# Issuing the first units of a layer stack beside the last pairs of the stage before it, with memory pools split by lifetime and weight loads moved to another queue

## The chip, the cores and the metric

The kernel runs on one core of a Trainium2 chip. The time is device time in microseconds (us). The core has five engines, each with its own in-order queue of instructions: TensorE (PE, matrix products; its weight loads are listed apart as PEld), VectorE (DVE), ScalarE (ACT), GpSimd (POOL) and SyncE (SP), which issues DMAs. ACT can issue DMAs too. All order between engines comes from semaphores: an instruction at the head of a queue waits, and everything behind it on that engine waits as well.

## What is computed

The input x is 16 sequences of 256 tokens by 128 features, in float32. Four residual blocks follow, cut here to what matters:

```python
x = x + attention(layernorm(x))        # 16 heads of 8, causal softmax
x = x + mixture(layernorm(x))          # per sequence: 2 of 8 rank-64 experts
x = x + retention(layernorm(x))        # 4 heads, decay matrix, rms norm, silu gate
x = x + stack(layernorm(x))            # 6 layers
# stack, per layer:
#   x = local_attention(shift(x)) + x  # 16 heads of 64, window 32, q and k normalised and rotated
#   x = feed_forward(shift(x)) + x     # layer norm, gelu gate
```

## The kernel before

**First stage.** The first three blocks work on pairs of sequences, 8 pairs (class First, g = 0 to 7). Each method is one step of a pair: `st`, `rs`, `z`, `tr`, `zt` (L184 to L227) are the layer norm and the transposition, with a letter for the block (a, m, r, and s for the stack's input); `pr`, `na`, `dq` (L234 to L248) project q and k and bring them into head order by way of DRAM; `sc` to `ov` (L266 to L387) are the attention; `oat` to `ax` (L389 to L404) its output projection and the addition to `xn`; `mxz` to `am` (L408 to L512) the mixture; `rpq` to `ar` (L516 to L678) the retention. `st` with letter s also saves xn to DRAM (`kept`, L186), and `zt` with letter s writes the pair into `xs` (L227), which the stack works on.

**Stack.** 6 layers by 16 sequences make 96 units (class Unit). A unit's steps are `pqk`, `sq`, `t2`, `rot`, `add` (L899 to L927: q and k of head group G, their squares, the rotation), `nr`, `rnA` to `rnC`, `bcD`, `norm` (L931 to L974: norms of q and k, broadcast through DRAM), `pv`, `vc`, `vs` (values), `s`, `sm`, `mx`, `sub`, `exp`, `su`, `rec`, `nm` (scores and softmax), `pt`, `pTc`, `o`, `oTc`, `y`, `xsu` (output). Class Forward does the feed-forward of a pair.

**Order.** Both stages run in an order that is written out by hand: the lists FIRST (L785) and ORDER (L1252). A word such as `oat:-1` is a step and an offset: in round j it is done for pair j - 1 (in ORDER, for unit 2j - 1). All steps are issued in this order, each to its engine's queue, so the list fixes every queue. FIRST is run for j = -8 to 15, and only then ORDER for j from -3, so the first stage's last rounds hold only steps of pairs 6 and 7, and the stack's first rounds only steps of units 0 to 3.

**Memory.** All first-stage tiles live in four pools (`xp`, `ew`, `wk`, and PSUM pools), opened together in one block (L727) and closed together after FIRST. The stack's pools `lw`, `kc`, `s2` (L818 to L820) take the same memory afterwards: `lw` holds weights of q and k, values' weights and rotation tables, `kc` the other weights, the ring of q and k tiles and the values, `s2` the working tiles.

**Loads.** SP loads the 8 tiles of x (L732); ACT loads constants and weights of the first stage, 15 DMAs (L126, L749, L753, L709), in program order ahead of ACT's first computation. POOL makes the scaled rotation tables a half at a time during FIRST (`tab`, L720), SP moves them. The stack's weights for layer 0 are issued by SP at L1299 to L1304; those of later layers by `follow` (L1277). Fills of tiles for attention (qT, kT, vals, less) stand at L758 to L775.

Of the kernel before, what the change touches and what calls it, by code (L numbers as in the profile page):

```python
# [105 lines left out]
_EARLY = ["mask0", "rcos", "rsin", "decay", "expand", "before"]  # L106
_LATE = ["ident", "band", "gather"]
# [3 lines left out]
def kernel(ctx: ExitStack, tc: tile.TileContext, a: dict, widths: dict, out: bass.AP):  # L111
# [12 lines left out]
    def load_consts(pool, names, array):  # L124
        whole = pool.tile([P, sum(widths[n] for n in names)], F32, name=f"c_{names[0]}")
        nc.scalar.dma_start(out=whole, in_=array)  # L126
        got, at = {}, 0
        for n in names:
            got[n] = whole[:, at : at + widths[n]]
            at += widths[n]  # L130
        return got

    c = load_consts(const, _LATE, a["late"])
    ident = c["ident"]
# [3 lines left out]
    def transposed(z, name):  # L138

        ps = bank(ps_tr, f"tr_{name}")  # L140
        for k in range(4):
            nc.tensor.transpose(ps[:, k * P : (k + 1) * P], z[:, k, :], ident)
        return ps
# [16 lines left out]
    class First:  # L160
# [9 lines left out]

        def bank(self, what, *n):
            return self.tile(ps_tr, [P, 512], what, *n, tag=ps_tr.name)
# [8 lines left out]
        def t_z(self, K):  # L181
            return self.wk([P, 4, D], "z", K, tag="ln_za" if K == "a" else "ln_z", bufs=1 if K == "a" else 2)

        def st(self, K):  # L184
            if K == "s":
                nc.sync.dma_start(out=kept[self.g], in_=xn[self.g])  # L186
            st, mv = self.wk([P, 4, 6], "ln_st", K, bufs=4), self.mv(K)
            for k in range(4):
                nc.vector.bn_stats(st[:, k, :], xn[self.g][:, k, :])
                nc.vector.bn_aggr(mv[:, k, :], st[:, k, :])  # L190

# [25 lines left out]
        def zT(self, K):  # L217
            return self.wk([P, 512], "zT", K, tag=f"zT_{K}", bufs=1)
# [18 lines left out]
        def nat(self, x):  # L237
            return self.wk([P, 512], "nat", x, tag=f"nat_{x}", bufs=1)
# [11 lines left out]
        def pav(self):  # L250
            zT = self.zT("a")
            for k in range(4):
# [26 lines left out]
        def mx(self, s, ch, r):  # L279
            for tt in range(2):  # L280
                cols = slice(P, 3 * P) if tt else slice(0, P)
                junk = self.wk([P, 2 * P], "a_junk", s, ch, r, tt, bufs=1)
# [19 lines left out]
        def qS(self, s, ch):  # L302
            return self.wk([P, T], "a_qS", s, ch)
# [23 lines left out]
        def e(self, s, ch, half):  # L327
            return self.wk([P, 3, 2, P], "a_pe", s, ch, half, bufs=4)
# [33 lines left out]
        def oT(self, s):  # L362
            return self.wk([P, 4, T], "a_oT", s)
# [14 lines left out]
        def ov(self, s, tt):  # L378
            p3 = self.bank("ta", s, tt).rearrange("t (h d) -> t h d", d=32)
            rec = self.wk([P, H0, 1], "a_rec", s, tt)  # L380
# [135 lines left out]
        def rpq(self, s):  # L516
            for tt in range(2):
# [188 lines left out]
    def scale_tables(pool):  # L706

        qks = pool.tile([P, DEPTH, 2, 2], F32, tag="qks", bufs=1, name="qks")
        nc.scalar.dma_start(out=qks, in_=a["qks"].rearrange("p (l k h) -> p l k h", l=DEPTH, k=2))  # L709
# [16 lines left out]
    xn = []  # L726
    with ExitStack() as early:  # L727
        xp = early.enter_context(tc.tile_pool(name="xp", bufs=1))
        ew = early.enter_context(tc.tile_pool(name="ew", bufs=1))
        for g in range(NPAIR):  # L730
            xt = xp.tile([P, 4, D], F32, name=f"xn{g}")
            nc.sync.dma_start(out=xt, in_=x_tok[g])  # L732
            xn.append(xt)
        w = load_consts(ew, _EARLY, a["early"])
        for name, shape, src in (
            ("wq", [P, P], a["wq0"]),
            ("wk", [P, P], a["wk0"]),
            ("wv", [P, P], a["wv0"]),
            ("wo", [P, P], a["wo0"]),
            ("wr", [P, NE], a["wr"]),  # L740
            ("wa", [P, 4, D], a["wa"].rearrange("(c p) h -> p c h", p=P)),
            ("wb", [P, 4, D], a["wb"].rearrange("(c p) h -> p c h", p=P)),
            ("wqk", [P, 2 * P], a["wqk1"]),
            ("wvg", [P, 4 * P], a["wvg1"]),
            ("wo1", [P, 2, D], a["wo1"].rearrange("(c p) n -> p c n", p=P)),
            ("gn", [P, 1], a["gn"]),
        ):
            w[name] = ew.tile(shape, F32, name=f"w_{name}")
            nc.scalar.dma_start(out=w[name], in_=src)  # L749


        w["ninth"] = ew.tile([P, 1], F32, name="ninth")
        nc.scalar.dma_start(out=w["ninth"], in_=a["ninth"])  # L753
        headed = {}
        for name in ("wq", "wk"):
            headed[name] = [dram.tile([P, 512], F32, name=f"heads_{name}{n}") for n in range(2)]
        w["qT"], w["kT"] = [], []
        for n in range(2):  # L758
            for kind in ("qT", "kT"):
                t = ew.tile([P, 4, 512], F32, name=f"a_{kind}{n}")  # L760
                if kind == "qT":
                    nc.vector.memset(t, 0.0)
                else:
                    nc.vector.tensor_copy(
                        t.rearrange("p c n -> p (c n)"), w["ninth"].to_broadcast([P, 4 * 512])
                    )
                w[kind].append(t)
        w["vals"] = ew.tile([P, 4, H0, 32], F32, name="vals")
        nc.gpsimd.memset(w["vals"][:, :, :, D0:], 0.0)
        nc.gpsimd.memset(w["vals"][:, :, :, D0 : D0 + 1], 1.0)  # L770
        w["less"] = []
        for n in range(2):
            t = ew.tile([P, 2, 4, 4, 32], F32, name=f"less{n}")
            nc.gpsimd.memset(t, 0.0)
            w["less"].append(t)  # L775

        nc.scalar.mul(w["gn"], w["gn"], 0.5)
        ps_s = early.enter_context(tc.tile_pool(name="ps_sa", bufs=1, **psum))
        ps_p = early.enter_context(tc.tile_pool(name="ps_pa", bufs=1, **psum))
        ps_tr = early.enter_context(tc.tile_pool(name="ps_ma", bufs=2, **psum))  # L780
        wk = early.enter_context(tc.tile_pool(name="wk", bufs=2))
# [3 lines left out]
        FIRST = """  # L785
        dc.1.1:-2 ex.1.3.0:-1 rs.a:2 sp.1.3.1:-1 wt.1.0:-2 af.1.2.1:-1 wt.1.1:-2 mx.0.2.1:0 ex.1.3.1:-1 os.1.0:-2
        oa.1.2:-1 os.1.1:-2 af.1.3.1:-1 af.1.3.0:-1 mx.0.2.0:0 sp.0.0.1:0 oa.1.3:-1 nd.1:-2 oc.1.2:-1 npw.0:-2 pav:0
        oc.1.3:-1 dv.1.0:-1 vlc:0 mx.0.2.2:0 tr.a:1 mx.0.2.3:0 ov.1.0:-1 ex.0.0.1:0 gm.0.0:-2 dv.1.1:-1 sc.0.3:0
        sp.0.0.0:0 ov.1.1:-1 mx.0.3.1:0 nmu.0:-2 zt.a:1 mx.0.3.2:0 tab.0:0 ex.0.0.0:0 gm.1.0:-2 mt.0.2:0 oat:-1
        sh.0.2:0 mx.0.3.3:0 mt.0.1:0 sh.0.1:0 onc:-1 ya:-1 mx.0.3.0:0 sp.0.1.0:0 ex.0.1.0:0 af.0.0.1:0 gm.1.1:-2  # L790
        npw.1:-2 ax:-1 sc.1.0:0 nmu.1:-2 st.m:-1 af.0.0.0:0 ont.0:-2 ont.1:-2 mx.1.0.1:0 af.0.1.0:0 onm.0:-2 rs.m:-1
        onm.1:-2 sp.0.2.1:0 yr:-2 ex.0.2.1:0 z.m:-1 tr.m:-1 sp.0.1.1:0 zt.m:-1 mx.1.0.0:0 mx.1.0.2:0 ar:-2 pl:-1 lg:-1
        oa.0.0:0 pr.q:1 mx.1.0.3:0 sc.1.1:0 af.0.2.1:0 ex.0.1.1:0 oc.0.0:0 mxz:-1 sp.0.2.0:0 ch1:-1 exq:-1 ch2:-1
        mx.1.1.0:0 st.s:-2 pg:-1 na.q:1 mx.1.1.3:0 gt:-1 dq.q:1 pe:-1 gc:-1 wg:-1 pr.k:1 na.k:1 mt.0.3:0 pm:-1
        ex.0.2.0:0 z.a:2 sh.0.3:0 mx.1.1.1:0 rs.s:-2 mt.1.0:0 sh.1.0:0 af.0.1.1:0 mx.1.1.2:0 mix:-1 tab.1:0 ym:-1
        z.s:-2 oa.0.1:0 sp.0.3.1:0 ex.0.3.1:0 af.0.2.0:0 am:-1 oa.0.2:0 st.r:-1 sp.0.3.0:0 sc.1.2:0 rs.r:-1 oc.0.1:0
        mx.1.2.0:0 oc.0.2:0 ex.0.3.0:0 z.r:-1 mt.1.1:0 sp.1.0.0:0 tr.r:-1 sh.1.1:0 dq.k:1 tr.s:-2 mx.1.2.2:0 zt.r:-1
        af.0.3.0:0 mx.1.2.3:0 af.0.3.1:0 mx.1.2.1:0 pvg.0:-1 zt.s:-2 rpq.0:-1 tv.0:-1 gg.0:-1 rt.0:-1 sc.1.3:0
        pvg.1:-1 mx.1.3.3:0 mx.1.3.1:0 pvg.2:-1 ex.1.0.0:0 tv.1:-1 gg.1:-1 ra.0:-1 tv.2:-1 sp.1.0.1:0 oa.0.3:0
        ex.1.0.1:0 oc.0.3:0 gg.2:-1 rpq.1:-1 rqt.0:-1 rqc.0:-1 sp.1.1.0:0 af.1.0.1:0 mx.1.3.0:0 mx.1.3.2:0 af.1.0.0:0  # L800
        rt.1:-1 raw.0.0:-1 sc.0.0:1 ex.1.1.0:0 sp.1.1.1:0 ex.1.1.1:0 dc.0.0:-1 raw.0.1:-1 dc.0.1:-1 wt.0.1:-1
        mx.0.0.2:1 os.0.1:-1 oa.1.0:0 mt.1.2:0 oc.1.0:0 af.1.1.0:0 mx.0.0.1:1 mx.0.0.3:1 tab.2:0 mx.0.0.0:1 ra.1:-1
        sh.1.2:0 rqt.1:-1 gm.0.1:-1 pvg.3:-1 rqc.1:-1 mt.1.3:0 st.a:3 sp.1.2.0:0 sh.1.3:0 tv.3:-1 ex.1.2.0:0
        af.1.2.0:0 af.1.1.1:0 sc.0.1:1 gg.3:-1 wt.0.0:-1 sp.1.2.1:0 mt.0.0:1 os.0.0:-1 mx.0.1.0:1 mx.0.1.1:1 dv.0.1:0
        sh.0.0:1 ex.1.2.1:0 ov.0.1:0 dv.0.0:0 ov.0.0:0 mx.0.1.2:1 oa.1.1:0 sp.1.3.0:0 oc.1.1:0 mx.0.1.3:1 raw.1.0:-1
        sc.0.2:1 dc.1.0:-1 nd.0:-1 raw.1.1:-1
        """.split()
        pairs = [First(g) for g in range(NPAIR)]
        tables = scale_tables(wk)
        with tc.manual_schedule():  # L810
            next(tables)
            for j in range(-8, NPAIR + 8):
# [565 lines left out]
```

## Time and profile before

| what | value |
|---|---|
| median of 3 timed runs | 4303.77 us (4298.45 to 4316.04) |
| profiled execution, its own time | 4305.45 us |
| its span, first to last instruction | 4303.7 us |
| TensorE busy, whole span | 4048.4 us (94%), 100320 matmuls |
| VectorE busy | 2947.2 us (68%) |
| ScalarE busy | 2077.9 us (48%) |
| GpSimd busy | 2525.9 us (59%) |
| mean granted TensorE clock | 0.964 |
| chain that ended last, by engine | PE 74%, DVE 6%, DMA 6%, POOL 4%, ACT 3%, issue 3%, SPq 3% |
| DMA read from HBM, written | 140.98 MB, 17.83 MB |

How to read it: the profile covers one execution. A row of a timeline or group gives the start, the duration, the engine, the source line, the operation and the tiles (output <- input); in brackets stands how long the engine had been idle and what released it. ACTq and SPq are DMA issues on ACT's and SP's queues. PEclk is the share of full speed that TensorE's clock was granted. A wait for several semaphores is put down to the one that came last by the profile. Matmul ends are modelled, so a busy PE is not a PE at its peak.

### The profile page before, as it was taken

Reading aid. Unit: us, or ns where it says so; the run is one execution under the profiler, and the core shown is the slowest. Engines: PE = TensorE matmul, PEld = TensorE weight load, DVE = VectorE, ACT = ScalarE, POOL = GpSimd, SP = SyncE. Lnnn points to the kernel's source line nnn. Section 1 sums busy time; section 2 is a strip of 40 time slices with the busy share of each in tenths; the row PEclk is TensorE's granted clock in tenths of the full one; section 3 lists DMA queues with packets and bytes.
Section 4 is the critical chain, followed back from the end, with each engine's and each line's share of the span. In section 5 each row is a group of like instructions: output and inputs, shape, how many; then the busy total and the mean of one; then the engine's idle time right before and its main releaser. Section 6 shows DMA issues by size and latency. Waiting matters only on the chain.

```text
span 4303.7 us, 216382 instructions
## 1 busy us (share of the span) xinstructions
PE 4048.4 (94%) x100320; PEld 2778.6 (65%) x100320; DVE 2947.2 (68%) x5436; ACT 2077.9 (48%) x3342; POOL 2525.9 (59%) x1419
## 2 busy tenths in 40 slices
PE   5999967999999999999999999999999999999998
PEld 3666654666666666666666666666666666666664
DVE  4677635677777677777777676766767776767764
ACT  2555532445554455544555544544554554445543
POOL 2454536666666666666666666666656666656661
PEclk9999977899999999999999999999999999999999
DMA  3111101222222222222222212222222222222221
GB/s 88 52 36 53 36 34 52 69 59 64 56 73 49 71 59 65 69 64 74 60 65 57 69 48 74 59 64 69 61 49 69 67 57 69 64 64 68 59 63 46
DMA packets 208899, 260.84 MB, mean 61 GB/s; under 512 B 54142, under 2 KB 164604, under 8 KB 207100
## 3 DMA queue, kind: packets, MB, share of 16 engines
q1 hardware_dynamic: 204796, 243.38, 22.1%
q8 instruction: 786, 12.88, 1.3%
q10 hardware_dynamic: 3200, 3.62, 0.3%
q14 instruction: 117, 0.96, 0.1%
HBM read 140.98 MB, written 17.83 MB: 37 GB/s over the span
## 4 chain that ended last, share of the span: by engine, by line
PE 74%; DVE 6%; DMA 6%; POOL 4%; ACT 3%; issue 3%; SPq 3%; ACTq 0%; POOLq 0%; DVEq 0%
PE pqk L902 14%; PE s L1014 11%; PE o L1092 9%; PE pv L980 8%; PE y L1111 5%; DMA v<-v 5%; PE nr L936 4%; PE pt L1069 3%; PE fy L1220 3%; PE fa L1203 3%; PE fg L1190 3%; POOL qk L974 2%; PE p L319 2%; SPq L967 1%; SPq L996 1%
## 5 line engine op out<-in xcount | busy, mean ns | idle before, releaser
L927 POOL TENSOR_TENSOR qk<-qk,t 128x1024 f32<-128x1024 f32 x384 | 907.3, 2366 | 303.1 <-DVE qk L921 301.9
L974 POOL TENSOR_TENSOR qk<-qk,bc 128x1024 f32<-128x1024 f32 x384 | 947.2, 2484 | 75.4 <-DMA v<-v 63.4
L1045 POOL TENSOR_TENSOR sm<-sm,mx 128x1024 f32<-128x1024 f32 x192 | 367.2, 1912 | 975.4 <-DVE mx L1041 291.8
L902 PE MATMUL pqk<-xs,wqk 128*128 128x256 f32 x3072 | 852.8, 406 | 23.0 <-ACT sq L910 12.3
L1014 PEld LDWEIGHTS s<-qk 32*32 32x32 f32 x49152 | 537.8, 104 | 400.5 <-issue 375.4
L910 ACT ACTIVATE sq<-pqk 128x512 f32<-128x512 f32 x768 | 454.6, 599 | 690.0 <-DVE qk L921 361.9
L916 DVE TENSOR_TENSOR t<-pqk,rot 128x512 f32<-128x512 f32 x768 | 521.9, 686 | 298.7 <-ACT sq L910 146.9
L921 DVE TENSOR_TENSOR qk<-pqk,rot 128x512 f32<-128x512 f32 x768 | 515.4, 682 | 278.0 <-PE pqk L902 222.7
L1014 PE MATMUL s<-qk 32*32 32x64 f32 x49152 | 667.8, 223 | 19.5 <-issue 7.6
L902 PEld LDWEIGHTS pqk<-xs,wqk 128*128 128x128 f32 x3072 | 547.8, 195 | 149.2 <-issue 50.1
L1092 PEld LDWEIGHTS o<-pT,v 64*64 64x64 f32 x24576 | 423.2, 139 | 295.0 <-issue 164.8
L1092 PE MATMUL o<-pT,v 64*64 64x32 f32 x24576 | 474.5, 224 | 78.4 <-DMA v<-v 76.3
L1077 ACT COPY pT<-pt 128x512 f32<-128x512 f32 x384 | 224.8, 586 | 449.1 <-PE pt L1069 238.2
L980 PE MATMUL pv<-wv,xs 128*64 128x512 f32 x1536 | 423.1, 630 | 0.0
L1063 DVE TENSOR_TENSOR sm<-sm,rec 128x1024 f32<-128x1024 f32 x192 | 404.2, 2105 | 0.0
L1111 PE MATMUL y<-oT,wo 128*128 128x256 f32 x1536 | 386.8, 396 | 0.3 <-ACT pT L1077 0.3
L1030 DVE TENSOR_TENSOR sm<-s,c_ident 128x1024 f32<-128x1024 f32 x192 | 234.1, 1219 | 148.7 <-PE s L1014 147.7
L1111 PEld LDWEIGHTS y<-oT,wo 128*128 128x128 f32 x1536 | 282.0, 193 | 43.9 <-ACT f_gl L1196 0.8
L1104 ACT COPY oT<-o 128x512 f32<-128x512 f32 x384 | 216.3, 590 | 164.1 <-PE o L1092 164.1
L989 ACT COPY v<-pv 128x512 f32<-128x512 f32 x384 | 224.7, 585 | 127.6 <-PE pv L980 127.5
L1053 DVE TENSOR_REDUCE su<-sm 128x16 f32<-128x1024 f32 x192 | 232.6, 1211 | 41.2 <-ACT sm L1049 41.2
L1069 PE MATMUL pt<-c_ident,sm 128*128 128x128 f32 x1536 | 249.3, 285 | 1.2 <-DVE f_res L1247 0.8
(187 smaller groups left out, 4983.6 us busy)
## 6 DMA issues: line engine op xcount, KB each, us to landing
bc<-ndr SPq DMA_DIRECT2D x768, 128.0 KB
v<-v SPq DMA_DIRECT2D x576, 128.0 KB
v<-v SPq DMA_DIRECT2D x192, 64.0 KB
rot_l<-in_rot_dram SPq DMA_DIRECT2D x12, 512.0 KB
rot<-rot_l SPq DMA_DIRECT2D x12, 512.0 KB
wqk<-in_wqk_dram SPq DMA_DIRECT2D x24, 256.0 KB
rot<-rot SPq DMA_DIRECT2D x6, 1024.0 KB
wv<-in_wv_dram SPq DMA_DIRECT2D x6, 512.0 KB
```

The costliest lines, as they stand in the source:

```text
L902: nc.tensor.matmul(self.p_qk(G, k)[:, hf, :], lhsT=weights["qk", G, self.l][:, k, hf, :], rhs=xq, start=True, stop=True)
L910: nc.scalar.activation(self.squares(G)[:, k], self.p_qk(G, k), AF.Square)
L916: nc.vector.tensor_tensor(self.t_2(G)[:, k], self.p_qk(G, k)[:, ::-1, :], weights["rot", self.l][:, 1, k], ALU.mult)
L921: nc.vector.tensor_tensor(self.qk_t[G][:, k, :, WIN : WIN + T], self.p_qk(G, k), weights["rot", self.l][:, 0, k], ALU.mult)
L927: nc.gpsimd.tensor_tensor(to, to, self.t_2(G), ALU.add)
L974: nc.gpsimd.tensor_tensor(to, to, self.bcast()[:, G, :, None, :].to_broadcast([P, 2, 2, T]), ALU.mult)
L980: nc.tensor.matmul(self.misc("pv", i)[64 * p : 64 * p + 64, :], lhsT=xs[self.g][:, self.seq, cols], rhs=weights["v", self.l][:, p, :], sta ...
L1014: nc.tensor.matmul(ps[32 * b : 32 * b + 32, r2, tt, G // 2, G % 2, :], lhsT=qk[G][rows, 0, hf, WIN + at : 2 * WIN + at], rhs=keys, start=( ...
L1063: nc.vector.tensor_tensor(s3, s3, self.t_rec(hu)[:, :, None].to_broadcast([P, 16, 2 * WIN]), ALU.mult)
L1069: nc.tensor.transpose(pt[:, j * P : (j + 1) * P], sm[:, j // 2, tt, j % 2].rearrange("n p c -> n (p c)"), ident)
L1092: nc.tensor.matmul(o[64 * e : 64 * e + 64, p, 2 * hu + m, WIN * b : WIN * b + WIN], lhsT=self.v_t[rows, 1 - b % 2, 2 * tt + b // 2, 4 * hu ...
L1111: nc.tensor.matmul(self.misc("y")[:, 0:T], lhsT=weights["o", self.l][:, ch, :], rhs=self.t_oT()[:, ch, :], start=(ch == 0), stop=(ch == 7),)
```

## The change

It does four things.

1. **Pools by lifetime.** What only the first attention uses (the x tiles of pairs 0 to 5, wq, wk, wv, mask0, qT, kT, vals, less, z, zT and nat of letter a, a_junk, a_qS, a_pe, a_oT, a_rec, rot_l) goes into pools `ea` and `aw`, the rest of the first stage stays in `ew` and `wk`. `ea`, `aw` and the attention's two PSUM pools are closed after the last attention step, and the stack's `lw` and `s2` are opened in their place, at the other end of memory. The ring of q and k moves into `lw`; values' weights, odd layers' rotation table, vals, wo, w1, w2 and vecs are in `kc`, a few working tiles in the new `s3`; both open when `ew` and `wk` close. The two-bank PSUM pool `ps_m` is opened at the start and serves both stages.
2. **A bridge.** FIRST runs up to the last attention step (`ov.1.1` of pair 7). The 104 steps left, of pairs 6 and 7, are issued in a new list BRIDGE together with 116 steps of units 0, 1 and 2. `ORDER` then skips what has been issued.
3. **Loads.** ACT issues only ident, ninth and mask0 (and no vecs later); SP issues x of pair 0, wq, wk, wv, x of pairs 1 and 2, then the rotation table. The other tiles of x and all other weights and constants of the first stage are issued by SP when `pav` of pair 0 is issued (`load_rest`).
4. **Fills.** Three of the four fills of qT and kT come after `st.a` of pair 0 (`set_heads`); the halving of gn comes at pair 0's `rpq`.

The core of the diff:

```diff
         def st(self, K):
...
+            if K == "a" and self.g == 0:
+                set_heads()
...
         def pav(self):
             zT = self.zT("a")
+            if self.g == 0:
+                load_rest()
...
         def rpq(self, s):
+            if self.g == 0 and s == 0:
+
+                nc.scalar.mul(w["gn"], w["gn"], 0.5)
...
+    early = ExitStack()
+    attention = ExitStack()
+    ew = early.enter_context(tc.tile_pool(name="ew", bufs=1))
+    wk = early.enter_context(tc.tile_pool(name="wk", bufs=2))
+    ea = attention.enter_context(tc.tile_pool(name="ea", bufs=1))
+    aw = attention.enter_context(tc.tile_pool(name="aw", bufs=2))
+    ps_s = attention.enter_context(tc.tile_pool(name="ps_sa", bufs=1, **psum))
+    ps_p = attention.enter_context(tc.tile_pool(name="ps_pa", bufs=1, **psum))
...
+    xn = [(ea if g < NPAIR - 2 else ew).tile([P, 4, D], F32, name=f"xn{g}") for g in range(NPAIR)]
+    nc.sync.dma_start(out=xn[0], in_=x_tok[0])
+    load(ea, nc.scalar, "ninth", [P, 1], a["ninth"])
+    load(ea, nc.scalar, "mask0", [P, 3 * P], a["mask0"])
+    load(ea, nc.sync, "wq", [P, P], a["wq0"])
+    load(ea, nc.sync, "wk", [P, P], a["wk0"])
+    load(ea, nc.sync, "wv", [P, P], a["wv0"])
+    nc.sync.dma_start(out=xn[1], in_=x_tok[1])
+    nc.sync.dma_start(out=xn[2], in_=x_tok[2])
+
+    def load_rest():
+
+        for g in range(3, NPAIR):
+            nc.sync.dma_start(out=xn[g], in_=x_tok[g])
+        load(ew, nc.sync, "wo", [P, P], a["wo0"])
+        load(ew, nc.sync, "wr", [P, NE], a["wr"])
+        w.update(load_consts(ew, _EARLY, a["early"]))
...
+        c.update(load_consts(const, _LATE, a["late"]))
...
+    nc.vector.memset(w["qT"][0], 0.0)
+
+    def set_heads():
         for n in range(2):
...
+            if n:
+                nc.vector.memset(w["qT"][n], 0.0)
+            nc.vector.tensor_copy(
+                w["kT"][n].rearrange("p c n -> p (c n)"), w["ninth"].to_broadcast([P, 4 * 512])
+            )
...
+    firsts = [
+        (method, args, j + d) for j in range(-8, NPAIR + 8) for method, args, d in parse(FIRST) if 0 <= j + d < NPAIR
+    ]
+    mine = ("sc", "mx", "mt", "sh", "sp", "ex", "af", "oa", "oc", "dv", "ov")
+    split = 1 + max(n for n, (method, _, _) in enumerate(firsts) if method in mine)
+
+    with tc.manual_schedule():
+        next(tables)
+        for method, args, g in firsts[:split]:
+            getattr(pairs[g], method)(*args)
+    del firsts[:split]
+    assert next(tables, None) is None
+    attention.close()
...
+    right = dict(side="right")
+    lw = ctx.enter_context(tc.tile_pool(name="lw", bufs=1, **right))
+    s2 = ctx.enter_context(tc.tile_pool(name="s2", bufs=2, **right))
...
+    BRIDGE = """
+        pqk.1.0:0 first.nmu.0:6 first.oat:7 pqk.1.1:0 t2.1.0:0 first.onc:7 first.gm.1.0:6 first.ya:7 first.gm.1.1:6
+        sq.1.1:0 t2.1.1:0 first.npw.1:6 rot.1.0:0 first.ont.0:6 first.ax:7 first.onm.0:6 rot.1.1:0 sq.1.0:0 pqk.0.1:0
+        pqk.0.0:0 first.st.m:7 first.nmu.1:6 first.ont.1:6 rot.0.1:0 sq.0.1:0 first.rs.m:7 first.onm.1:6 t2.0.1:0
+        first.yr:6 add.1:0 t2.0.0:0 first.z.m:7 pqk.3.1:0 rot.0.0:0 first.ar:6 sq.3.1:0 first.tr.m:7 first.mxz:7
+        sq.0.0:0 rot.3.1:0 pqk.3.0:0 t2.3.1:0 first.zt.m:7 first.pl:7 sq.3.0:0 pqk.2.1:0 add.0:0 t2.3.0:0 first.lg:7
+        first.ch1:7 t2.2.1:0 first.exq:7 rot.3.0:0 first.ch2:7 first.st.s:6 first.pg:7 first.gt:7 first.pe:7
+        first.gc:7 rot.2.1:0 pqk.2.0:0 sq.2.1:0 first.wg:7 sq.2.0:0 t2.2.0:0 rot.2.0:0 nr.0:0 first.rs.s:6 first.pm:7
+        add.3:0 pqk.1.1:1 first.mix:7 first.z.s:6 nr.1:0 rnA:0 pqk.0.0:1 t2.1.1:1 first.ym:7 rnB:0 rnC:0 first.am:7
+        bcD:0 sq.0.0:1 rot.1.1:1 sq.1.1:1 pqk.1.0:1 add.2:0 first.st.r:7 rot.0.0:1 first.rs.r:7 t2.0.0:1 t2.1.0:1
+        rot.1.0:1 pqk.0.1:1 first.z.r:7 add.1:1 sq.1.0:1 pqk.3.1:1 rot.0.1:1 first.tr.r:7 first.tr.s:6 first.zt.r:7
+        first.zt.s:6 first.pvg.0:7 norm.1:0 t2.0.1:1 rot.3.1:1 first.tv.0:7 first.rpq.0:7 sq.0.1:1 first.gg.0:7
+        norm.0:0 pqk.3.0:1 first.rt.0:7 first.pvg.1:7 t2.3.0:1 first.tv.1:7 first.pvg.2:7 t2.3.1:1 first.ra.0:7
+        rot.3.0:1 sq.3.1:1 s.0.0.0:0 first.gg.1:7 first.tv.2:7 add.0:1 first.rpq.1:7 sq.3.0:1 first.gg.2:7 pqk.2.1:1
+        first.rt.1:7 first.rqt.0:7 sq.2.1:1 pqk.2.0:1 norm.3:0 first.rqc.0:7 sq.2.0:1 first.ra.1:7 first.raw.0.0:7
+        first.dc.0.0:7 norm.2:0 s.0.1.0:0 t2.2.1:1 first.raw.0.1:7 rot.2.1:1 pqk.1.0:2 first.dc.0.1:7 first.wt.0.1:7
...
+        rnA:1 rnB:1 rnC:1 pqk.1.1:2 s.0.0.1:0 s.0.1.1:0 first.nmu.1:7 sm.0:0 bcD:1 s.1.0.0:0 add.3:1 first.ont.1:7
+        t2.1.0:2 sq.1.1:2 s.1.1.0:0 first.onm.1:7 t2.1.1:2 first.yr:7 rot.1.0:2 mx.0:0 add.2:1 s.1.0.1:0 rot.1.1:2
+        sq.1.0:2 first.ar:7 s.1.1.1:0 sub.0:0 pqk.0.1:2 first.st.s:7 exp.0:0 first.rs.s:7 norm.0:1 first.z.s:7
...
+    """.split()
...
     with tc.manual_schedule():
         for G in range(4):
             weights["qk", G, 0] = load_qk(0, G)
         weights["rot", 0] = load_rot(0)
+        for word in BRIDGE:
+            ((method, args, u),) = parse([word])
+            if method == "first":
+                getattr(pairs[u], args[0])(*args[1:])
+                firsts.remove((args[0], args[1:], u))
+            else:
+                getattr(units[u], method)(*args)
+                issued.add((u, method, *args))
+        assert not firsts
+    early.close()
+
+    kc = ctx.enter_context(tc.tile_pool(name="kc", bufs=1))
+    s3 = ctx.enter_context(tc.tile_pool(name="s3", bufs=2))
...
+    nc.sync.dma_start(out=vecs, in_=a["vecs"].rearrange("p (l n) -> p l n", l=DEPTH))
...
+    with tc.manual_schedule():
         weights["v", 0] = load_v(0)
...
             for method, args, d in parse(ORDER):
                 u = 2 * j + d
-                if 0 <= u < len(units):
+                if 0 <= u < len(units) and (u, method, *args) not in issued:
```

## The prediction

> All positions are microseconds in the profiled execution of before; that run took 4305.45 (span 4303.7), 1.7 above the median 4303.77 of the three timed runs, so differences carry over to the median unchanged.
>
> **What bounds the kernel now.** First the page's slices, because they show where TensorE is not the bound.
>
> ```profile
> PE   5999967999999999999999999999999999999998
> ...
> PEclk9999977899999999999999999999999999999999
> DMA  3111101222222222222222212222222222222221
> ```
>
> A slice is 107.6. PE is below nine tenths in the first slice, in the sixth and seventh (538 to 753), and at the end; its clock sags at the same places. So I asked for busy times by stage (columns: length, PE, weight loads, DVE, ACT, POOL, then granted clock, DMA share, GB/s).
>
> ```profile
> 0.00:20.00 20.00, 0.00 (x0) 0.00 (x0) 6.64 (x18) 0.00 (x0) 7.61 (x25) 1.00 0.98 293
> ...
> 568.00:640.00 72.00, 43.64 (x264) 31.44 (x263) 21.01 (x68) 21.45 (x54) 25.58 (x41) 0.70 0.05 15
> 640.00:706.50 66.50, 45.11 (x856) 30.90 (x856) 29.95 (x46) 15.85 (x25) 34.28 (x15) 0.76 0.27 82
> 706.50:746.00 39.50, 29.93 (x802) 20.64 (x801) 23.47 (x32) 14.00 (x21) 26.03 (x13) 0.80 0.23 53
> 746.00:800.00 54.00, 51.28 (x1432) 35.70 (x1428) 33.31 (x42) 23.37 (x38) 34.61 (x15) 0.83 0.16 41
> 800.00:4200.00 3400.00, 3310.03 (x90211) 2263.07 (x90208) 2434.74 (x3563) 1702.82 (x2596) 2135.93 (x957) 0.98 0.25 64
> ```
>
> From 800 on PE is busy 97% of the time: the stack is bound by TensorE and the change leaves its work as it is. Two stages are bound by latency. In 568 to 640 only the tail of pairs 6 and 7 runs, one dependent step after another; in 640 to 706.5 only the first units run, again a chain. No engine is busy over 68% in either. The first 20 have no matmul at all while DMA is at 0.98. Third, the timeline of ACT over the start, and of SP and ACT at the seam:
>
> ```profile
> 1.26 0.55 ACTq L126 DMA_DIRECT2D c_mask<-in_early_dram  x1
> ...
> 10.47 0.39 ACTq L749 DMA_DIRECT2D w_wq<-in_wq_dram  x1
> ...
> 20.38 0.44 ACTq L709 DMA_DIRECT2D qks<-in_qks_dram  x1
> 20.86 1.28 ACT L202 ACT_TABLE_LOAD   x1 [20.86 <-DMA w_wqk<-in_wqk_dram]
> 22.15 0.50 ACT L202 ACTIVATE z_a<-xn,ln_nb_a,ln_rs_a 128x128 f32<-128x128 f32 x1
> ...
> 637.47 1.13 ACT L227 COPY xs<-tr_s 64x256 f32<-64x256 f32 x3
> ```
>
> ACT issues loads until 20.8, and pair 0's first normalisation stands behind them in its queue, though its operands (POOL's L197) are ready at 9.25. At the other end, pair 7's last copy to xs ends at 638.6.
>
> ```profile
> 636.62 1.96 SPq L851 DMA_DIRECT2D wqk<-in_wqk_dram  x4
> 638.64 0.41 SPq L857 DMA_DIRECT2D rot<-rot  x1
> ...
> 641.31 3.60 PE L902 MATMUL pqk<-xs,wqk 128*128 128x256 f32 x8 [4.25 <-DMA wqk<-in_wqk_dram]
> ...
> 646.28 1.29 DVE L916 TENSOR_TENSOR t<-pqk,rot 128x512 f32<-128x512 f32 x2 [13.49 <-DMA wv<-in_wv_dram]
> ```
>
> SP issues the stack's weights only at 636.62, when ACT's z_s (ending 636.5), the last reader of xn, is done: the new pool waited for the whole old pool. First matmul 4.7 after the issue, first rotation 9.7 after it.
>
> **The start.** ACT keeps three small loads (ident, ninth, mask0), so its queue is free at about 2.5, and the table load is over by 4. What then holds z_a is x's first tile. It landed at 5.5, beside 1760 KB of constants; alone, by the nearest row (a 256 KB write of nat_q, issue 68.54, next step 70.56) it takes 2 to 3, so 3.8. Statistics 1.7 (5.50 to 7.19), POOL's four small steps 2.0 (7.28 to 9.25): z_a at 7.8, at worst 9.3. Gain 14.3 or 12.9; I take 14. The rest of that chain (22.15 to 38.98, first scores) is unchanged: set_heads puts 2.36 + 1.76 + 2.36 = 6.5 of DVE work behind pair 0's statistics, done at about 12, before the heads' DMA needs kT (now about 17) and pair 1's statistics are used. Attention's tiles only change their pool; buffer counts stay: nothing. The postponed loads (4,320 of the 6,060 KB, 15 at 293 GB/s) go to SP behind pair 0's heads, about 23 to 39; next on SP is pair 1's nat_q at 68.5 - 14 = 54. Cover 15; without it, up to 15 on that one DMA. Scaling gn costs 0.19 on ACT: nothing.
>
> [...] The row says more: between 1.8 and 10.47 ACT issued nothing while the transfers drained, and this blocked compute too. What counts is that two thirds of the bytes, and their waits, no longer stand ahead of z_a. I go by the row: 14.
>
> **The seam.** Attention's last read of its pools is ov.1.1 of pair 7, ending at 568.2. SP has nothing else queued (its last table write is at 544.7), so wqk and rot issue at 568.2 instead of 636.6: first matmul 572.9, first rotation 577.5 (rot now follows wqk directly). POOL's ring memsets, 1.2, wait for the same point. The order is static, so this wait has others behind it: on PE pair 7's oat behind pqk.1.0 (4.7 lost); on DVE pair 7's add to xn (ax) behind two t2 and a rot. ax was at 570.5 and goes to 577.5 + 3 x 0.65 = 579.5: the tail's chain starts 9 late.
>
> From there the chain is as before (570.5 to 638.6, 68), but each step also waits for unit work put ahead of it on its engine. Sums of what the bridge issues, from durations in these stages at full clock: PE 31 for units + 30 for pairs = 62; POOL 35 + 27 = 62 (14 adds and norms at 2.36 are 33); DVE 30 + 22 = 52; ACT 17 + 20 = 37. None is near 90, so the chain stays the limit. Walking it, delay against before grows thus: ax 9; ch1 11 (pqk.3.0 ahead of the router's product, t2 and rot on DVE); mix 12; am 13.5 (pqk.1.1, nr.1, pqk.0.0 ahead of ym, a PSUM bank held for the norms); tr.r 16 (pqk.3.1 waits for sq.1.0, which stands behind z.r); ra.0 16.5 (norm.1 and norm.0 ahead on POOL: they wait for the broadcast, 9 from rnC at 667.9 to norm at 676.9, which is about what the chain takes from am to ra.0, so this costs little); raw.0.1 21 (behind s.0.1.0, which waits for norm.2); ont.1 24 (nr.1, three groups of scores, one of them after sm.0 because its PSUM tile has one buffer, then a Sqrt table load of 1.28); the end 24. So pair 7 ends at 638.6 + 24 = 663.
>
> [...] The rows differ: 0.70 at 61% busy, 0.76 at 68%, but still only 0.83 at 95% busy (746 to 800). At 0.8 PE's 62 are 77; about half of PE's work is on the chain: +8. I take +4, between: 667.
>
> Then the second new wait. vecs and wv go into pools that open only when pair 7's is closed: issued at about 666, landed 4.7 later (the wqk row), so PE holds at pv.0 of unit 0 until 671, with everything behind it on PE. pv.0 and pv.3 take 2, and pqk.3.1 of unit 2 starts at 673. Before, the same instruction came at 706.5, also with these two pv done. Gain 33.5; POOL and DVE, which don't wait for wv, are then a few us further ahead (add.1 of unit 2 at about 668 against 706.7), worth 0 to 4. I take 34. SP issues wo and ff right behind (2.5 of issue, ahead of unit 2's broadcast, which is some 20 later); they land long before use: nothing. Steady state: same instructions, buffers and PSUM banks: nothing.
>
> Sum: -14 - 34 = -48: 4305.45 - 48 = 4257.5 by the profiled run, 4256 by the median.
>
> **Rivals.**
> 1. Loads find free memory before 568 or the clock stays full: the 9 at ax vanish, or the 4. Gain up to 14 + 47 = 61: 4243. For it: the free bytes at the top of memory aren't in the trace. Against: before's wqk waited for a whole pool.
> 2. The bridge's in-order queues cost more than my walk: 45 hops at 0.4 more each, 18. Gain 14 + 16 = 30: 4274.
> 3. The seam gives nothing and only the start remains: 4290. This is so if pair 7 ends at 701 or later.
> 4. Slower: the stack's first values, output weights and feed-forward must wait for pair 7's very end, because their pools lie where its tiles are. If the mixed queues lengthen that chain from 68 to 135 (1.5 more at each of 45 hops, as with a POOL add of 2.36 ahead of two steps in three), it ends at 714 and the start's gain is used up: break-even. At 736 it is slower by 0.5% (21.5, about what a measurement can tell from no change): 4326. Against it: only 14 adds and norms exist, and they total 33.
>
> **How the numbers follow.** My forecast (4256, within 4247 to 4265) 0.5; rival 1 0.17; rival 2 0.2; rival 3 0.08; rival 4 0.05. Faster by over 0.5% is below 4282: 0.87; within 0.5% 0.08; slower 0.05. The range takes in rivals 1 and 2: 4238 to 4278.
>
> **What would show it.** z_a at 8 to 9.5 and first scores near 25; wqk issued within 1 of pair 7's last ov, at about 554 on the new time axis; ax about 9 after where it stood relative to that; pair 7's last copy to xs some 95 to 100 after it; PE waiting about 5 for wv at the first pv; from there on the old timeline, 48 early. I'd be wrong if first-stage time between first scores and ov changed (529 now), if the stretch 800 to 4200 changed, or if the chain grew by a POOL or PSUM wait that I priced at nothing.

## The result, and the profile after

The changed kernel takes 4277.4 us (median of 5 runs, 4273.91 to 4286.27) against 4303.77 (5 runs, 4298.45 to 4317.93): ratio 0.9935, 95% interval 0.991 to 0.9959. The gain is 26 us, 18 to 39 by the interval; 48 was forecast. The profiled execution took 4277.4, its span is 4275.7.

First the slices of the changed kernel's page. TensorE in slice 1 rose from 5 to 6 tenths, in the dip of slices 6 and 7 from 6 and 7 to 7 and 8:

```profile
PE   6999978999999999999999999999999999999998
```

The same columns by stage (length, PE, weight loads, DVE, ACT, POOL, granted clock, DMA share, GB/s) for the start and the mixed tail:

```profile
0.00:20.00 20.00, 5.40 (x8) 1.89 (x8) 8.73 (x20) 5.90 (x12) 11.37 (x25) 1.00 0.34 102
557.70:654.50 96.80, 71.45 (x1112) 55.11 (x1112) 50.50 (x116) 37.83 (x80) 56.30 (x53) 0.84 0.19 51
```

The DMA share at the start fell from 0.98 to 0.34, and GpSimd's busy time rose from 7.61 to 11.37 with the same 25 instructions: that is the first thing not forecast. In the mixed tail TensorE is busy 74% of the time at a granted clock of 0.84; before, the same place had 61% at 0.70.

The timeline of the start in the changed kernel shows where GpSimd's time went:

```profile
5.61 1.20 DVE L792 COPY a_kT<-w_ninth 128x2048 f32<-128x2048 f32 x1
5.78 1.11 POOL L203 TENSOR_SCALAR ln_rs_a<-ln_mv_a 128x4 f32<-128x4 f32 x1 [1.01 <-DVE ln_mv_a L197]
6.97 3.93 POOL L204 TENSOR_TENSOR ln_rs_a<-ln_rs_a,mhalf 128x4 f32<-128x4 f32 x1
7.18 1.76 DVE L791 MEMSET a_qT<- 128x2048 f32 x1 [0.37 <-issue]
8.86 1.17 DVE L792 COPY a_kT<-w_ninth 128x2048 f32<-128x2048 f32 x1
11.55 1.65 ACT L211 ACTIVATE z_a<-xn,ln_nb_a,ln_rs_a 128x128 f32<-128x128 f32 x4 [6.22 <-POOL ln_nb_a L206]
```

Two operations on 128 x 4 elements take 1.11 and 3.93, while DVE runs the three moved fills; before, with no fill beside them, the same two took 0.23 and 1.04:

```profile
7.28 0.23 POOL L194 TENSOR_SCALAR ln_rs_a<-ln_mv_a 128x4 f32<-128x4 f32 x1 [2.51 <-DVE ln_mv_a L190]
7.60 1.04 POOL L195 TENSOR_TENSOR ln_rs_a<-ln_rs_a,mhalf 128x4 f32<-128x4 f32 x1
```

So z_a starts at 11.55 (22.15 before), not at 7.8.

The seam, on the changed kernel's timeline:

```profile
557.92 1.78 SPq L871 DMA_DIRECT2D wqk<-in_wqk_dram  x4
...
567.98 1.29 DVE L935 TENSOR_TENSOR t<-pqk,rot 128x512 f32<-128x512 f32 x2 [10.25 <-PE ont L221]
569.78 0.67 DVE L240 TENSOR_TENSOR xn<-xn,ya 128x512 f32<-128x512 f32 x1
...
653.02 1.50 ACT L236 COPY xs<-tr_s 64x256 f32<-64x256 f32 x4
...
653.47 0.42 SPq L882 DMA_DIRECT2D wv<-in_wv_dram  x1
...
657.58 3.68 PE L999 MATMUL pv<-wv,xs 128*64 128x512 f32 x8 [4.60 <-DMA wv<-in_wv_dram]
```

wqk is issued 0.2 after the last ov ends at 557.73. Pair 7's addition (the xn row) starts 12.0 after that end, and its last copy to xs ends 96.8 after it. TensorE then waits 4.60 for wv. The forecast had 11.3, 98.8 and 5 for these three.

What was not: in the stack TensorE's one large wait grew. The waits of PE between the first pT copy of unit 8 and that of unit 92 (us in total, times, longest), before:

```profile
PE o L1092 <- DMA v<-v: 65.5, 80, 3.5
```

and after:

```profile
PE o L1111 <- DMA v<-v: 82.9, 89, 3.8
```

Both executions, cut at four marks (the end of the last ov, and the first copy to pT of units 0, 8 and 92), with a second trace of each kernel taken later (us):

| stretch | before | after | gain | before again | after again | gain |
|---|---|---|---|---|---|---|
| start to last ov | 568.2 | 557.7 | 10.5 | 570.6 | 556.1 | 14.5 |
| to unit 0 | 147.9 | 109.4 | 38.5 | 150.6 | 109.3 | 41.3 |
| to unit 8 | 303.4 | 299.1 | 4.3 | 294.6 | 300.1 | -5.5 |
| to unit 92 | 3124.6 | 3155.5 | -30.9 | 3117.3 | 3121.1 | -3.8 |
| to the end | 159.6 | 154.0 | 5.6 | 151.5 | 153.9 | -2.4 |
| span | 4303.7 | 4275.7 | 28.0 | 4284.7 | 4240.5 | 44.2 |

Start and seam gave what was promised, and more; 31 of it was lost between units 8 and 92 in the first pair of traces, 4 in the second.

### The profile page after: what moved, and what is told of

Read it like the earlier page. It is cut to its first block, busy times and chain, and to the rows that moved or that the text cites. A ratio compares the mean times of both kernels' runs of the same rounds, so it can differ in the third digit from the quotient of the medians.

```text
span 4275.7 us, 216376 instructions
## 1 busy us (share of the span) xinstructions
PE 4036.9 (94%) x100320; PEld 2776.4 (65%) x100320; DVE 2940.5 (69%) x5436; ACT 2077.0 (49%) x3344; POOL 2527.3 (59%) x1419
## 4 chain that ended last, share of the span: by engine, by line
PE 68%; DMA 9%; DVE 8%; POOL 6%; ACT 4%; issue 3%; SPq 3%; POOLq 0%; ACTq 0%; DVEq 0%
PE pqk L921 13%; PE s L1033 10%; PE o L1111 9%; PE pv L999 7%; DMA v<-v 6%; PE y L1130 5%; PE nr L955 4%; PE fy L1239 3%; PE pt L1088 3%; POOL qk L993 3%; PE fg L1209 2%; PE fa L1222 2%; PE p L330 2%; DVE sm L1082 1%; SPq L986 1%
## 5 line engine op out<-in xcount | busy, mean ns | idle before, releaser
L1111 PE MATMUL o<-pT,v 64*64 64x32 f32 x24576 | 480.0, 225 | 94.8 <-DMA v<-v 91.8
L1049 DVE TENSOR_TENSOR sm<-s,c_band 128x1024 f32<-128x1024 f32 x192 | 233.9, 1218 | 145.2 <-PE s L1033 144.2
L1088 PE MATMUL pt<-ident,sm 128*128 128x128 f32 x1536 | 247.1, 284 | 1.8 <-issue 1.0
```

Of the source, the lines that this page charges most:

```text
L1088: nc.tensor.transpose(pt[:, j * P : (j + 1) * P], sm[:, j // 2, tt, j % 2].rearrange("n p c -> n (p c)"), ident)
L1111: nc.tensor.matmul(o[64 * e : 64 * e + 64, p, 2 * hu + m, WIN * b : WIN * b + WIN], lhsT=vals[self.u % 2][rows, 1 - b % 2, 2 * tt + b // 2 ...
```

## Experiments

The experiments ran in four later comparisons, in which the kernel before took 4275.8 to 4286.1 instead of 4303.77; so ratios, and differences within a comparison, are compared. Where "the stretch" is named, it is that from unit 8 to unit 92.

**The moved fills.** One move: they come with pair 1's statistics.

```diff
-            if K == "a" and self.g == 0:
+            if K == "a" and self.g == 1:
                 set_heads()
```

> The changed kernel with one move: set_heads (three fills of qT and kT on DVE) comes after st.a of pair 1 instead of pair 0. Theory 'fills slow POOL': z_a at 7.8 to 8 instead of 11.55, POOL's power step about 1.05 instead of 3.93, time 3.7 less: about 4273.7. Rival 'x lands late': z_a stays within 1 of 11.55, time 4277. The stretch from unit 8's to unit 92's first copy to pT is the same program as in the changed kernel: it should be 3155 again (3124.6 before the change) if the steady-state loss belongs to the program, anything else within 15 if it is chance of one execution.

The timeline of this kernel:

```profile
6.25 1.04 POOL L204 TENSOR_TENSOR ln_rs_a<-ln_rs_a,mhalf 128x4 f32<-128x4 f32 x1
7.93 1.65 ACT L211 ACTIVATE z_a<-xn,ln_nb_a,ln_rs_a 128x128 f32<-128x128 f32 x4 [2.45 <-POOL ln_nb_a L206]
...
9.66 3.95 POOL L204 TENSOR_TENSOR ln_rs_a<-ln_rs_a,mhalf 128x4 f32<-128x4 f32 x1
...
11.55 1.16 DVE L792 COPY a_kT<-w_ninth 128x2048 f32<-128x2048 f32 x1
```

z_a starts at 7.93, the first scores at 24.74 instead of 28.29. The slow power step moved along with the fills: now pair 1's takes 3.95, and again it ends 0.9 after the last fill (13.61 and 12.71; in the changed kernel 10.90 and 10.03). So the fills hold GpSimd up. The time is 4249.49, ratio 0.9913 (0.989 to 0.9937); the 3.6 are clear in the trace, but the timed runs can't tell them from the changed kernel's own 0.9918. The stretch is 3126.8, not 3155: the first sign that the loss there was no fixed property of the program.

**Placement by 32 bytes.** In the changed kernel lw and s2 begin 32 bytes past a multiple of 64 per partition; before, bc and the ring were on multiples. In its first trace the DMAs also landed later after their issue (up to the 16th landing that follows, in the mean of the stretch: v<-v 3.91 instead of 3.66, bc<-ndr 4.25 instead of 4.16; the expectation has 0.25 and 0.15 for the differences). An unused tile moves the addresses, first in the kernel before:

```diff
+    gap = ctx.enter_context(tc.tile_pool(name="gap", bufs=1))
+    gap.tile([P, 8], F32, name="gap")
     s2 = ctx.enter_context(tc.tile_pool(name="s2", bufs=2))
```

> The kernel before with an unused tile of 32 bytes per partition ahead of pool s2, nothing else: s2's tiles, bc among them, then begin 32 bytes past a multiple of 64, as in the changed kernel. Theory 'placement': bc's broadcasts land 0.15 and the shifts of v 0.25 later as in the changed kernel, the stretch from unit 8 to unit 92 grows from 3124.6 to about 3155, time about 4334. Rivals 'rhythm after the bridge' and 'chance': stretch 3125, time 4304.

4283.34, ratio 0.9995 (0.998 to 1.0009), stretch 3115.5: nothing. The same tile on the right side of the changed kernel, ahead of lw:

> The changed kernel with an unused tile of 32 bytes per partition at the far end of memory, ahead of lw: all tiles of lw and s2 (ring, bc, sq, weights of q and k) begin at multiples of 64 again. Theory 'placement by 32 bytes': stretch from unit 8 to unit 92 back to 3125, time about 4247. Rival 'rhythm', or placement in another sense (which half of memory): stretch 3155, time 4277.

4244.9, ratio 0.991 (0.9894 to 0.9926), stretch 3122.7. Read alone, this looks like a hit. But without that tile the variant with the later fills has 3126.8, and the changed kernel itself, in the next experiment, 3121.1: the theory of 32 bytes falls.

**Both kernels again, unaltered.**

> The changed kernel once more, unaltered. Theory 'the steady-state loss belongs to the program': stretch from unit 8's to unit 92's first copy to pT again about 3155 and 30 more than in the kernel before taken beside it. Rival 'most of the 31 was chance of two executions': about 10 more than before's, as in the three variants of the changed kernel (3122.7 to 3126.8, against 3115.5 for before with the gap), and a gain of 35 to 40 in the timed runs instead of 26.

> The kernel before once more, for a second trace of its stretch from unit 8 to unit 92. Theory 'program': 3125 or 30 less than the changed kernel beside it. Rival 'chance': 3110 to 3120 and about 10 less than the changed kernel beside it.

The changed kernel: 4250.68, ratio 0.9918 (0.9895 to 0.9941), a gain of 34; stretch 3121.1, beside 3117.3 in the kernel before (4286.4). This trace is of the fastest of the six runs (4242.25), so its loss is likely below the usual: the timed gain of 34 is still 15 short of the 49 that start and seam give. The waits in it, kernel before and changed kernel:

```profile
PE o L1092 <- DMA v<-v: 61.3, 70, 3.5
```

```profile
PE o L1111 <- DMA v<-v: 67.9, 77, 4.0
```

So the 31 lost in the stack is not a constant of the program. The clock's records give the second part. In those of the first two traces (96 before, 94 after) the clock is granted whole or half, in stretches of 3.41 or a multiple (but for the last of each, which runs past the last instruction); half the length of the half-clock stretches is counted as lost. Three terms then make up every trace:

| kernel | stretch | wait for v<-v | lost to half clock | rest |
|---|---|---|---|---|
| before | 3124.6 | 65.5 | 47.8 | 3011 |
| before again | 3117.3 | 61.3 | 42.7 | 3013 |
| after | 3155.5 | 82.9 | 61.4 | 3011 |
| after again | 3121.1 | 67.9 | 35.8 | 3017 |
| fills later | 3126.8 | 70.7 | 37.5 | 3019 |

In all eleven traces that have this wait, the rest is 3011 to 3019. The 31 are 17.4 more waiting and 13.6 more half clock. The two hang together: of 19 stalls of o over 1 us in the kernel before, 15 are followed within 8 by a stretch of half clock, of 20 in the changed one 18 (of points taken at random in the two stretches 8 and 10%). Of the 47.8 and 61.4 lost, 39 and 41 lie in half-clock stretches that begin within 8 after such a stall. Of the 33 stalls that half clock follows, 29 are shorter than 3.41.

**The bridge's list taken out.** The remaining steps of pairs 6 and 7 in their old order, the pools as changed:

```diff
-        for word in BRIDGE:
...
-        assert not firsts
+        for method, args, g in firsts:
+            getattr(pairs[g], method)(*args)
```

> The changed kernel with its pools and loads, but unmixed: the 104 steps of pairs 6 and 7 in their old order, then ORDER from its start. Seam: the tail is again 70 from pair 7's last ov to its last copy, with weights of q and k and the rotation table loaded already, so unit 0 starts about 4 to 5 earlier than before; the bridge's 34.8 less that is lost: seam gain 0 to 5 instead of 34.8. Theory 'placement': stretch from unit 8 to unit 92 still 3155, time 4304 - 10.5 - 5 + 30 = 4319. Rival 'rhythm after the bridge': stretch 3125, time 4289.

4271.92, ratio 0.9965 (0.9951 to 0.9979). The expectation rested on an unmixed order, and the timeline shows that this kernel is not unmixed:

```profile
561.11 2.10 PE L683 MATMUL yr<-w_wo,r_oT 128*128 128x128 f32 x16
563.04 0.60 PE L921 MATMUL pqk<-xs,wqk 128*128 128x256 f32 x2
...
564.37 0.71 PE L221 MATMUL tr_m<-ident,z_m 128*128 128x128 f32 x2 [0.73 <-ACT z_m L211]
```

Unit 0's products stand between two steps of the pairs, though the lists have them behind the last step of pair 7: it seems that, once the pools are open, the building of the program moves steps of one list into the end of the list before. So the run compares the written mix with one made by the build. The tail lasts 81.4 and unit 0's first copy to pT comes 136.9 after the last ov; with BRIDGE these are 96.8 and 109.4, before 70.4 and 147.9. Of the 38.5 gained up to there, the pools alone bring 11, the written order 27.5. The stretch is 3126.7 again.

**The weights that TensorE waits for.**

```diff
-        w = kc.tile([P, 2, 512], F32, tag="wv", bufs=2, name=f"wv{l}")
+        w = (kc if l % 2 else lw).tile([P, 2, 512], F32, tag="wv", name=f"wv{l}")
...
         weights["rot", 0] = load_rot(0)
+        weights["v", 0] = load_v(0)
...
-        weights["v", 0] = load_v(0)
         weights["o", 0] = load_o(0)
```

> The changed kernel with the values' weights of even layers in lw instead of kc, so that those of layer 0 load right behind the first rotation table instead of after pair 7's last step. If the 4.6 that TensorE waits for them at the first pv is a loss of its own: that wait is gone and the time is 4 to 5 less. Rival: the tiles that pv's copies write still lie in the pool that opens after pair 7, so TensorE stops a little later at the next pv for a PSUM bank, and the gain is 0 to 2.

4244.53, ratio 0.9897 (0.987 to 0.9923), against 0.9918 without: the sign is right, but the size lies inside the intervals. In the trace the first pv starts at 651.63 without the wait, unit 8 is reached 402.2 after the last ov instead of 408.5 to 411.5 in four traces with the change's own seam and ORDER (after, after again, fills later, the 32-byte tile).

**Pair 7's addition first.** The words oat, onc, ya, ax of pair 7 move to the head of BRIDGE:

```diff
-        pqk.1.0:0 first.nmu.0:6 first.oat:7 pqk.1.1:0 t2.1.0:0 first.onc:7 first.gm.1.0:6 first.ya:7 first.gm.1.1:6
-        sq.1.1:0 t2.1.1:0 first.npw.1:6 rot.1.0:0 first.ont.0:6 first.ax:7 first.onm.0:6 rot.1.1:0 sq.1.0:0 pqk.0.1:0
+        first.nmu.0:6 first.oat:7 first.onc:7 first.gm.1.0:6 first.ya:7 first.gm.1.1:6 first.npw.1:6 first.ax:7
+        pqk.1.0:0 pqk.1.1:0 t2.1.0:0
+        sq.1.1:0 t2.1.1:0 rot.1.0:0 first.ont.0:6 first.onm.0:6 rot.1.1:0 sq.1.0:0 pqk.0.1:0
```

> The changed kernel with pair 7's oat, onc, ya, ax and pair 6's steps among them issued ahead of unit 0's first products, so that nothing of the units stands ahead of pair 7's addition. If the late start of the tail's chain is the biggest term of the seam (ax 12.0 after the last ov, 2.3 before the change): ax about 3 after the last ov, pair 7's last copy some 88 after it instead of 97, unit 0's first copy to pT 5 to 9 earlier, time 5 to 9 less. Rival: the units' chain ends last in the seam, not pair 7's; then the last copy moves but unit 0's first copy to pT stays within 2.

4251.59, ratio 0.9916 (0.9892 to 0.994): nothing. On DVE:

```profile
560.11 0.69 DVE L240 TENSOR_TENSOR xn<-xn,ya 128x512 f32<-128x512 f32 x1 [2.25 <-PE ya L412]
567.99 1.29 DVE L935 TENSOR_TENSOR t<-pqk,rot 128x512 f32<-128x512 f32 x2 [7.20 <-DMA rot<-rot]
...
570.39 0.28 DVE L196 BATCH_NORM_STATS2 ln_st_m<-xn 128x6 f32<-128x128 f32 x1
```

The addition is 9.7 earlier, and the tail still lasts 97.3: the next step of the chain, pair 7's statistics, stands behind the same t2 and rot, which wait for the rotation table. The wait moved by one step, so the run did not show what the tail's late start is worth.

**The wait for v.** One unit of the changed kernel's second trace, from the last copy into its v to the o that reads it:

```profile
1372.12 0.59 ACT L1008 COPY v<-pv 128x512 f32<-128x512 f32 x1 [1.11 <-PE pv L999]
...
1382.67 0.37 SPq L980 DMA_DIRECT2D ndr<-rn  x1
...
1385.31 4.71 SPq L986 DMA_DIRECT2D bc<-ndr  x8
...
1390.13 5.61 SPq L1015 DMA_DIRECT2D v<-v  x8
1394.47 0.42 PE L1111 MATMUL o<-pT,v 64*64 64x32 f32 x2 [2.71 <-DMA v<-v]
```

The values are there at 1372.7, but their shift is issued from 1390.13, because vs.0 stands in SP's queue behind the nine DMAs of a later unit's broadcast. Of the 17.4 between, SP issues nothing for the first 9 (what stands ahead isn't ready), then two loads of weights; the broadcast takes the last 7.5. Two words of ORDER put it ahead of them, in both kernels:

```diff
-        ... vc.1:1 su.1:1 ... pTc.1.1:1 vs.0:1 oTc.1.1:0 ...
+        ... vc.1:1 vs.0:1 su.1:1 ... pTc.1.1:1 oTc.1.1:0 ...
-        ... vc.1:2 nr.0:4 ... t2.1.0:5 vs.0:2 rot.1.0:5 ...
+        ... vc.1:2 vs.0:2 nr.0:4 ... t2.1.0:5 rot.1.0:5 ...
```

> The changed kernel with vs.0 of a unit issued ahead of the next-but-one unit's bcD on SP's queue (in ORDER vs.0:1 follows vc.1:1, and vs.0:2 follows vc.1:2), nothing else. TensorE's one large wait in the stack is o for the transfers v<-v (69 to 86 between units 8 and 92), most of it for vs.0, which stands behind the nine DMAs of a broadcast. Theory 'the stack gives time back through this wait, and through the half-clock windows that its stalls bring on': the wait falls to 10 to 30, the stretch from unit 8 to unit 92 by 40 to 70, time about 4190 to 4210 where the changed kernel takes 4250. Rival: the broadcast now lands later and POOL's norms, then TensorE's scores, wait for it instead: stretch within 15 of 3124.

4178.61, ratio 0.9773 (0.9749 to 0.9796): 62 less than the changed kernel by the ratios. The stretch is 3071.5, 50 less than in the changed kernel's second trace. PE's waits in it, now:

```profile
PE pqk L921 <- DVE qk L940: 28.7, 34, 2.0
PE trf L1190 <- DVE ln_z L1184: 22.7, 36, 1.9
...
PE s L1033 <- POOL qk L993: 5.5, 7, 2.8
```

The wait for v<-v is gone, and the clock loses 13.7 instead of 35.8 to 61.4; part returns as waits for DVE (6.2 and 3.4 in the second trace of the changed kernel). The rival's wait for the broadcast is the last row, 5.5.

> The kernel before with the same two moves of vs.0. If the difference between the two kernels in the stack is only this wait, then with the wait gone from both, the gain of the change is what start and seam give, 11 + 38 = 49, instead of 34: the time is about 49 above that of the changed kernel with the same moves, 4240 to 4260. Rival 'other cause in the stack': the difference stays at about 34 to 40.

4231.63, ratio 0.9893 (0.9867 to 0.9919), so the same two words are worth 46 here. Without the wait the two kernels stand 53 apart by the medians; by the ratios (0.9893 - 0.9773) x 4279.29 = 51, give or take 15. That fits the 49 of start and seam, but leaves the rival's 36 to 40 just inside. The two traces fit it less well. They are only 28 apart (spans 4187.7 and 4215.8; the first is of the slowest of its four runs, the second of the fastest), and the stretch is 3071.5 in the changed kernel against 3058.4, 13 longer. Of these 13, 11 are more waiting for DVE, by the sums of the two rows pqk and trf (51.4 against 40.4):

```profile
PE pqk L902 <- DVE qk L921: 25.0, 24, 2.0
PE trf L1171 <- DVE ln_z L1165: 15.4, 33, 0.6
```

So the wait for v need not be all that the change loses in the stack.

**Placement as a whole.** The kernel before, its order and loads untouched, with every tile of the stack in SBUF where the changed kernel has it (the banks in PSUM, which the change shifts too, stay as before):

```diff
-    lw = ctx.enter_context(tc.tile_pool(name="lw", bufs=1))
-    kc = ctx.enter_context(tc.tile_pool(name="kc", bufs=1))
-    s2 = ctx.enter_context(tc.tile_pool(name="s2", bufs=2))
+    right = dict(side="right")
+    lw = ctx.enter_context(tc.tile_pool(name="lw", bufs=1, **right))
+    s2 = ctx.enter_context(tc.tile_pool(name="s2", bufs=2, **right))
+    kc = ctx.enter_context(tc.tile_pool(name="kc", bufs=1))
+    s3 = ctx.enter_context(tc.tile_pool(name="s3", bufs=2))
...
-        t = kc.tile([P, 2, 2, WIN + T], F32, name=f"qk{n}")
+        t = lw.tile([P, 2, 2, WIN + T], F32, name=f"qk{n}")
```

> The kernel before with the changed kernel's places in memory for all tiles of the stack (lw and s2 at the far end with the ring in lw; values, their weights, odd rotation tables and the other weights in kc, the last working tiles in s3), its order, loads and seam untouched. Theory 'placement costs a little in the stack': TensorE's wait for v<-v 69 instead of 63 and the stretch from unit 8 to unit 92 about 7 longer than 3116, time 4292. Rival 'placement does nothing': wait and stretch as before, time 4285.

4281.69, ratio 1.001 (0.9992 to 1.0028), wait for v 62.2, stretch 3120.6. If placement in SBUF costs anything, it is under 12.

**All three moves.** The fills later, wv early and vs.0 first, on the changed kernel:

> The changed kernel with the three moves together: fills of qT and kT behind st.a of pair 1, values' weights of even layers in lw and loaded behind the first rotation table, and vs.0 ahead of bcD. If the terms add up: 3.6 less at the start and 4 to 6 less at the seam on top of the kernel with vs.0 first (4178.6), so 4168 to 4172. Rival: with the wait for v gone the stack is nearer to its VectorE and GpSimd, and the earlier start of unit 0 is given back: 4175 to 4180.

4177.6, ratio 0.9761 (0.9736 to 0.9787): the same as vs.0 alone, within the intervals, and where the rival put it. z_a is at 7.85 and TensorE doesn't wait for wv, but unit 8 comes 405.9 after the last ov (406.9 with vs.0 alone), so of the two small moves only the start's is seen. Both this kernel and the one with vs.0 alone beat the kernel before and the changed one.

## Why the prediction was right in part

- **Sign and place: right.** Both bounds named (loads ahead of z_a, the pools' release at the seam) were the ones that gave way. But 4277.4 lies outside the forecast's own 4247 to 4265, and inside the wider range by less than 1; the range went that far for rival 2, whose mechanism did not act. That is luck.
- **The start: a cost in the sum was too small.** Forecast 14, measured 10.6 (22.15 - 11.55). The tile of x came at 4.00 (forecast 3.8), and the statistics took 1.7 as forecast. The term that failed is "POOL's four small steps 2.0": they took 5.7 (5.78 to 11.52). The step behind it reads "set_heads puts 2.36 + 1.76 + 2.36 = 6.5 of DVE work behind pair 0's statistics": it was weighed against kT and pair 1, not against GpSimd's steps of pair 0, which lie on the path. With the fills moved, z_a is at 7.93 and the gain 14.2. The 6.5 is a misread row as well: 2.36 is the time of both copies, merged in one row of before. The fills themselves took 1.20 + 1.76 + 1.17 = 4.1.
- **The seam: right, with the parts in other proportions.** Tail of pair 7 forecast 98.8 after the last ov (663 + 4 - 568.2), measured 96.8 and 97.1; wait for wv forecast 5, measured 4.6. The walk holds on the trace: the delay against before is 9.8 at ax (forecast 9), 12.3 at ch1 (11), 14.8 at mix (12), 16.3 at am (13.5), 20.4 at ra.0 (16.5) and 26.4 at the end (24, and 4 for the clock). The first rotation came 10.1 after wqk's issue, not 9.3: in the rows of before, too, rot follows wqk directly, so nothing was to be gained there. At pqk.3.1 of unit 2 the changed kernel is 45.3 ahead, less 10.5 from the start: 34.8, forecast 34. For the clock the sum added 4, between the walk as it stands (94.8) and 8 more by the rows of before (102.8); the tail lies between the two. But no run shows the full clock that 94.8 supposes: the granted clock in the tail was 0.84 and 0.86, near the 0.8 of the rows. (In the slices of before it sags in 6 to 8 alone, not in the first and the last, where PE is low as well.) The experiment on ax shows that its delay is not a term of its own: statistics wait for the same rotation.
- **The steady state: this step failed.** "Steady state: same instructions, buffers and PSUM banks: nothing." It was -31 in the first trace and -4 in the second. The same instructions don't mean the same time here: some 65 of the stretch are waits for a transfer behind a queue, and 39 to 48 more are half clock, most of it after such stalls; both vary from one execution to the next. The page of before already named this wait as TensorE's largest; a term priced at nothing should have had its size as the bound.
- **Not all of that loss is chance.** The four kernels with the change's seam and the wait that were timed later (after again, fills later, the 32-byte tile, ax first) have ratios of 0.991 to 0.9918: 35 to 39 us gained of the 49 or more, with intervals that end at 45 to 47. In the traces the stretch is 3129 in the mean of seven traces with the change's pools (3113.9 to 3155.5) and 3119.5 in that of four with the old order and loads (3115.5 to 3124.6). Of these 9, 7 are a longer wait for v (69.9 against 62.6) and 1 is half clock.
- **The rivals.** The gain of 26 lies near rival 2's 30, but not by its mechanism: the bridge's queues cost no more than the walk. The slower rival had no part.
- **Open.** Why the wait for v is longer in the changed kernel is not settled. The new places in SBUF alone don't bring it (wait 62.2, and under 12 in time), and it is there without the written order too (71.8 in the run without BRIDGE). The PSUM banks (the prediction has "same", but the change shifts them), the loads and the moment at which the units enter the stack were not tried by themselves. Nor is it known why the wait was 83 in the first trace; the five runs of that comparison lie close together (4273.91 to 4286.27), so it was hardly one odd execution, but the ratios of the first comparison and of the later ones don't differ beyond their intervals.

## What to carry to other kernels

Before a gain at the edges of a kernel is booked, look at the steady state for a wait that varies: it can take back much of such a gain (31 of 49 in the first traces here), and one pair of traces can't tell its chance part from the change's own effect. When work is moved, ask of each engine on the path what runs beside it then, not only whether its queue is free (here a GpSimd step of 1.04 took 3.93 while VectorE's fills ran). A DMA that is ready early but issued behind a broadcast is cheap to find: compare the end of its input's writing with its issue; here two words of the order were worth 62 in the changed kernel and 46 in the one before, more than the whole change.

## What the runs showed of the hardware

- GpSimd's operation on 128 x 4 elements, 1.04 alone (before), lasted 3.93 (changed kernel) and 3.95 (fills later, pair 1) while VectorE filled 128 x 2048 tiles, and ended 0.9 after the last fill. Beside VectorE's statistics (6.25 with the fills later) it took 1.04. The runs don't tell which of the fills, the memset or the copies, held it: the operation did not end in the 2.05 between the two copies (6.81 to 8.86), when only the memset ran, but GpSimd's own memset of less took 0.97 both beside a memset of VectorE (before) and without one (the changed kernel).
- In the first traces of both kernels TensorE's granted clock was whole or half, in stretches of 3.41 or a multiple, and stalls of o over 1 us were followed by half clock within 8 in most cases (15 of 19 before, 18 of 20 after), though 29 of these 33 were shorter than 3.41. In the first trace of the kernel before, 65.5 of waiting came with 47.8 of lost clock; with the wait gone (vs.0 first), 17.1 was lost.
